# Queries, maxima and normalised rows issued from ScalarE's DMA queue in a decoder-layer kernel

## The chip, the cores and the metric

The kernel runs on one core of a Trainium2 chip. Its engines are TensorE (PE, with PEld for the loading of weights), VectorE (DVE), ScalarE (ACT), GpSimd (POOL) and SyncE (SP); SP does no arithmetic here and issues transfers. A transfer between DRAM and the on-chip memory (SBUF), or within SBUF, is issued by an instruction of SP, ACT or POOL, which stands in the order of that engine's other instructions. The metric is the device time of one execution in microseconds (us); less is better. Three runs of the kernel before took 1378.53, 1389.58 and 1391.62 us, a median of 1389.58 us.

## The reference

The input x has 16 batches of 128 positions and 1024 channels in float32, and a context of the same shape goes with it. Three residual blocks follow each other, each behind a layer normalisation:

```
x = x + attention(layernorm(x))        # 32 query heads of 32, 8 key heads, rope, causal softmax
x = x + autocorrelation(layernorm(x), ctx, ctx)
x = x + mixed_streams(layernorm(x))
```

The autocorrelation takes the correlation of each channel with the context's by Fourier transforms, keeps the nine largest delays, and adds the context shifted by them with softmax weights. The last block splits the channels into four streams of 256 and computes, per position, logits for a 4x4 matrix, which 50 Sinkhorn iterations make doubly stochastic; the matrix mixes the four streams, and a small matrix product of their weighted sum is added.

## The kernel before, in words

**First part.** Projections and rope are computed for four batches at a time. What the second part needs is written to DRAM: rotated queries (`qd`) and keys (`kd`), each as two float32 tensors whose sum is exact (a "high" and a "low" part), values (`vd`), and the spectra of the context (`sd`).

**Second part.** A Python generator `batch(b)` records the work of one batch in pieces, and each `yield` gives the time until the next piece. A heap merges the 16 generators (and `fill()`, which adds the last spectra) by these times, `PERIOD` = 33 apart; the merged order is the priority that a scheduler then works with when it writes each engine's instructions in one fixed list. On the chip every engine runs its own list in that order. Nothing overtakes on an engine, a transfer's issue included: an issue that waits for a semaphore holds up all that stands behind it on the same engine.

**Attention of a batch**, in two halves f of sixteen heads:

- `keys(b)` (L396 to L402) loads 96 rows of keys into one of two fixed buffers, the rows high, low, high, in three transfers from SP.
- `queries(b, f)` (L404 to L410) takes a buffer `qs` (two are in rotation) and loads the rows high, high, low, in three transfers of 256 KB from SP (L409). A product over the 96 rows is then the score to full precision.
- `maxima` multiplies queries by keys (L421), takes each row's maximum on DVE (L428), turns the 128x16 maxima into 16x128 by a TensorE transpose (L432), negates them into a rounded part `nh` on ACT (L434) and a rest `nl` on DVE (L436), writes both to DRAM from SP (L438), and reads them back from there into rows 96 and 97 of `qs` (L439). So the next product can subtract the maximum by itself.
- `attended` multiplies again in the other direction, now over all 98 rows (L447), takes the exponential on ACT (L451), masks on POOL (L452), and then sums the weights (L460) and the weighted values (L464) on TensorE. `batch(b)` loads the values (L786) behind the maxima.

**The rest of a batch.** `projected_out` (L507 to L509, 48 matmuls) adds to the rows of x in `xt` (three buffers, loaded at L793). `cross` multiplies the context's spectra with those of a sequence: a matmul (L516), a load `sv` of 512 KB (L518, two buffers in rotation), two ACT copies (L520, L521), a product on DVE (L523) and two on POOL (L524, L525). `delays` uses it once and `delayed` twice per half of the channels, six loads for a batch; between them stands the search for the nine largest (L541 to L562) on DVE. `logits` stores the row sums (L590), normalises into `z` on ACT (L162, L167), stores `z` to DRAM from SP (L593), and computes the logits (L603 to L615). `branch` adds the small product to the output by an accumulating transfer from POOL (L657). `sinkhorn` and `mixed` work on groups of 7, 6 and 3 batches; `mixed` reads the stored `z` back (L740), mixes on TensorE (L753) and adds to the output from POOL (L766).

**The order around the change.** All loads and stores of the second part but the accumulating ones stand on SP's list. With its waits, a batch has there: three issues of keys, six of queries, six of maxima, six of `sv`, and one each of values, x, row sums and `z`. ACT's list holds transfers only ahead of the second part (constants and weights).

Of the kernel before, what the change touches and what calls it, by code (L numbers as in the profile page):

```python
# [11 lines left out]
FP = mybir.dt.float32  # L12
FR = mybir.dt.float32r
# [7 lines left out]
B, L, D = 16, 128, 1024  # batches, positions, channels  # L21
NK = D // 128  # chunks of 128 channels
HD, NH, NKV = 32, 32, 8  # attention: head size, query heads, key heads
TG = 4  # batches that share one projection
# [3 lines left out]
TOPK = 9  # int(2 * ln(128))  # L28
ITERS = 50
REFRESH = 7  # L30
# [3 lines left out]
# The order of the program: us between batches, and between the parts of one.  # L34
PERIOD = 33
T_S, T_MX, T_M, T_ST, T_PT, T_SUM, T_DIV, T_OUT = 0, 3.29, 13.22, 1.0, 2.56, 54.8, 422239.83, 5.08
T_LN, T_X, T_DEL, T_TOP, T_WT, T_X2, T_DLD = 7.24, 5, 0, 9.35, 3.53, 2.3, 1.0
T_Z, T_ZT, T_LT, T_LOG, T_XP, T_XPT = 15, 2.82, 0.76, 8.03, 14.22, 1.18
SKS, MIXS = [45.0, 257.52, 400.81, 8, 8, 8], [11.22, 56.61, 24.78, 4, 4, 4]
# [8 lines left out]
T_FILL, T_SPEC = 39.7, 24.48  # L48
# [5 lines left out]
# The constant matrices, each [128, 128], in the order in which they lie in the input "mats".  # L54
# [4 lines left out]
def constant_matrices():  # L59
    """Rope tables, causal mask, and the real Fourier matrices of 128 positions.  # L60

    Rows 0..63 of a spectrum are real parts and rows 64..127 imaginary ones. At the even
    frequencies (k / 128) row 0 is frequency 0 and row 64 is frequency 64, both real; the odd ones
    are (k + 1/2) / 128. With a spectrum V of the context and one Q of the other sequence,
    V[re, re] * Q + V[im, im] * [Q im, -Q re] holds the real parts of a cross spectrum and, below
    them, its imaginary parts; at row 0 and 64 of the even frequencies V[im, im] is zero and
    V[re, re] has the real value.

    Frequency 0 adds the same to every correlation of a channel. Neither their order nor their
    softmax depends on it, so that "g" leaves it out, and "f_c" can add to frequency 0 the 128 of  # L70
    the last value by which the even half of the delayed sums lacks half the last value.
    """
# [18 lines left out]
    # Of the values less the last one.  # L91
# [9 lines left out]
    # Row 32 s + i to column i.  # L101
# [4 lines left out]
def constant_tokens():  # L106
    """Of row 4 t + j, one in column t."""
    return np.repeat(np.eye(32, dtype=np.float32), 4, 0)
# [3 lines left out]
def tile_decoder(ctx: ExitStack, tc, x, cx, wqkv, wo, wlog, base, gate, wb, mats, toks, zero, eye4, out):  # L112
# [11 lines left out]
    # What the first part leaves to the second: rotated queries and keys in two exact parts each,  # L124
    # values, and the context's spectra (even re, even im, odd re, odd im; each twice, below each other).
    qd = [dram.tile([TG, 2, 4, 2, 128, 128], FP, name=f"qd{g}") for g in range(B // TG)]
# [4 lines left out]
    def rsqrt(v, eps):  # L131
        """1 / sqrt(v + eps), with a Newton step behind the tables."""
# [13 lines left out]
    def layernorm(o, i):  # L146
        """Into o; the variance and the factor too."""
# [9 lines left out]
    def layernorm_act(o, i, sums, norm):  # L157
        """The same on ScalarE, of the sums of two halves."""
# [13 lines left out]
    def over(a, n):  # L172
        """[128, m] -> [128, m, n]"""
        return a.unsqueeze(2).to_broadcast([128, a.shape[1], n])

    def repeat(a, n):
        """[128, m] -> [128, n, m]"""
        return a.unsqueeze(1).to_broadcast([128, n, a.shape[1]])

# [1 line left out]
    # The last spectra fill the beginning of the second part: what they need lies to the right.  # L181
# [3 lines left out]
    with ExitStack() as att:  # L185
# [12 lines left out]
        def weights(j, n):  # L198
            """A block of 256 columns, half of its rows."""
# [39 lines left out]
        def rotated(xh, xl, col, d):  # L239
            """Two chunks of features, of the first and the second halves of eight heads."""  # L240
# [38 lines left out]
        def tokens(g):  # L279
            """Begun before the projections of the group before it are done."""  # L280
# [14 lines left out]
        # Keys, values, then queries.  # L295
# [11 lines left out]
        for g in range(B // TG):  # L307
# [6 lines left out]
            for p in range(4):  # L314
                more_weights(2)
                rotated(xh, xl, p * 256, qd[g][:, :, p])
                more_spectra(SPEC[g][p])
                ahead = next(coming, None)

# [7 lines left out]
    def q_late():  # L327
        """What the first batch needs behind the last spectra."""
# [36 lines left out]
    # The ninth largest, and no others.  # L365
# [15 lines left out]
    # sigmoid(gate), and (1 - sigmoid(gate)) on the diagonal.  # L381
# [12 lines left out]
    max_d = [[dram.tile([2, 16, 128], FP, name=f"mx{b}_{f}") for f in range(2)] for b in range(B)]  # L394

    def keys(b):  # L396
        g, t = divmod(b, TG)
        ks = KS[b % 2]
        rows = kd[g][t].rearrange("i u (d h) t -> i (u d) (h t)", h=8)
        for r, i in enumerate((0, 1, 0)):  # L400
            SP.dma_start(out=ks[32 * r : 32 * r + 32, :].bitcast(FP), in_=rows[i])
        return ks  # L402

    def queries(b, f):  # L404
        g, t = divmod(b, TG)
        qs = q2.tile([98, 2, 1024], FR, name="qs")
        rows = qd[g][t, :, 2 * f : 2 * f + 2].rearrange("i p u (d h) t -> i (u d) p (h t)", h=8)
        for r, i in enumerate((0, 0, 1)):
            SP.dma_start(out=qs[32 * r : 32 * r + 32].bitcast(FP), in_=rows[i])  # L409
        return qs.rearrange("r p c -> r (p c)")  # L410
# [470 lines left out]
```

## Time and profile before

| what | us |
|---|---|
| median of three runs | 1389.58 |
| span of the profiled execution, first to last instruction | 1391.9 |
| first part, to about | 390 |
| attention of batches 0 to 15, first to last maxima transpose | 414.3 to 1091.3 |
| logits of the last batch written (L615) | 1213.0 |
| last mixed stream added from POOL (L766) issued | 1383.9 |

| engine | busy us | share of the span |
|---|---|---|
| PE | 1134.1 | 81% |
| DVE | 874.0 | 63% |
| POOL | 673.0 | 48% |
| ACT | 580.5 | 42% |

The profile was taken in one execution; its span of 1391.9 us is 0.3 us above the longest of the three runs, so that nothing has to be added for what lies around it. A line of code is written L421, and an arrow `a<-b` reads "a is written from b". A busy PE is not PE at its limit, since the ends of pipelined matmuls are modelled: neighbouring matmuls of L507 to L509 are listed with 0.39 us each and start 0.23 us apart. DMA queue 1 carries what SP issues, 199.99 MB of 221.78 MB; ACT's queue 10 carries 3.90 MB.

### The profile page before, as it was taken

The page shows a single profiled execution, that of the slowest core. Times are in us where ns is not written, and L with a number is a line of the kernel's source. Part 1 is how long each engine was busy: PE and PEld are TensorE (multiplying, and loading weights), DVE is VectorE, ACT ScalarE, POOL GpSimd, SP SyncE. Part 2 cuts the span into 40 slices and gives each one's busy share as a digit, 9 for nine tenths or more (in the row PEclk, how much of TensorE's full clock was granted, in tenths as well). Part 3 has the DMA queues.
Part 4 walks back from the last instruction along what each step waited for, and adds up shares of the span by engine and source line. Part 5 has one row for each costly group of instructions (what it writes and reads, how often), then busy time and mean ns, then how long its engine had stood idle before and what let it go on. Part 6 is the DMA issues. An engine that isn't in the chain of part 4 may idle for free.

```text
span 1391.9 us, 17636 instructions
## 1 busy us (share of the span) xinstructions
PE 1134.1 (81%) x5024; PEld 725.9 (52%) x5024; DVE 874.0 (63%) x2910; ACT 580.5 (42%) x1281; POOL 673.0 (48%) x813
## 2 busy tenths in 40 slices
PE   5999969989847999999999998999998976452232
PEld 3888748758623555645565555645564553231121
DVE  5463332321123466977788778968897999986840
ACT  3331221221223355557565666556555755321010
POOL 0353313223413365565566656676766766643332
PEclk9999989989956999999999999999999987655555
DMA  6662864765898444576556664476455444365265
GB/s 227 213 215 84 229 204 123 229 196 137 245 271 250 123 129 140 156 200 166 152 161 170 194 180 135 131 183 156 145 158 153 123 119 115 87 121 106 49 121 76
DMA packets 141824, 221.78 MB, mean 159 GB/s; under 512 B 23264, under 2 KB 86112, under 8 KB 141664
## 3 DMA queue, kind: packets, MB, share of 16 engines
q1 hardware_dynamic: 127936, 199.99, 49.1%
q0 software_dynamic: 10752, 16.78, 8.4%
q10 hardware_dynamic: 3040, 3.90, 0.9%
q8 instruction: 39, 0.64, 0.2%
q14 instruction: 57, 0.47, 0.1%
HBM read 129.93 MB, written 90.83 MB: 159 GB/s over the span
## 4 chain that ended last, share of the span: by engine, by line
PE 40%; DVE 27%; DMA 16%; issue 6%; ACT 4%; SPq 4%; POOL 3%; POOLq 0%; DVEq 0%; ACTq 0%
PE mm L249 4%; PE mm L247 4%; PE mm L248 4%; PE sm L460 4%; PE av L464 3%; PE ps L516 3%; DMA sv<-sd 3%; DMA out<-mx 2%; DVE mx L428 2%; PE o L507 2%; DVE kept L542 2%; DMA sd<-F 2%; PE ps L227 2%; PE o L508 2%; DVE P L523 2%
## 5 line engine op out<-in xcount | busy, mean ns | idle before, releaser
L524 POOL TENSOR_TENSOR s<-s,sv 128x512 f32<-128x512 f32 x96 | 125.2, 1305 | 64.6 <-ACT s L521 47.3
L753 PE MATMUL ps<-mz,hm 128*128 128x256 f32 x128 | 59.4, 622 | 97.5 <-POOL hm L745 71.9
L525 POOL TENSOR_TENSOR P<-P,s 128x512 f32<-128x512 f32 x96 | 125.9, 1313 | 13.3 <-DVE P L523 11.6
L247 PE MATMUL mm<-xh,wh 128*128 128x512 f32 x320 | 131.2, 412 | 0.0
L248 PE MATMUL mm<-xl,wh 128*128 128x512 f32 x320 | 126.6, 396 | 0.2 <-DVE xl L216 0.2
L249 PE MATMUL mm<-xh,wl 128*128 128x512 f32 x320 | 125.5, 392 | 0.0
L257 POOL TENSOR_TENSOR ra<-ra,rb 128x512 f32<-128x512 f32 x40 | 50.4, 1279 | 155.3 <-DVE rb L256 155.2
L507 PE MATMUL o<-woh,ch 128*128 128x512 f32 x256 | 108.9, 425 | 8.3 <-DVE xt L500 6.1
L452 POOL TENSOR_SCALAR_AFFINE_SELECT pt<-pt 128x512 f32<-128x512 f32 x128 | 83.7, 668 | 64.7 <-ACT pt L451 63.0
L508 PE MATMUL o<-woh,cl 128*128 128x512 f32 x256 | 106.8, 417 | 4.7 <-POOL cl L494 4.7
L421 PE MATMUL sc<-ks,qs 96*128 96x128 f32 x512 | 98.2, 323 | 10.1 <-DMA qs<-qd 10.1
L228 ACT COPY F<-ps 128x512 f32<-128x512 f32 x64 | 36.5, 585 | 158.5 <-DMA sd<-F 85.5
L509 PE MATMUL o<-wol,ch 128*128 128x512 f32 x256 | 101.9, 398 | 0.0
L428 DVE TENSOR_REDUCE mx<-sc 128x4 f32<-128x512 f32 x128 | 86.4, 680 | 23.7 <-PE sc L421 23.7
L421 PEld LDWEIGHTS sc<-ks,qs 96*128 96x128 f32 x512 | 82.4, 204 | 33.0 <-issue 26.6
L753 PEld LDWEIGHTS ps<-mz,hm 128*128 128x128 f32 x128 | 36.0, 305 | 120.7 <-POOL hm L745 82.0
L523 DVE TENSOR_TENSOR P<-sv,ps 128x512 f32<-128x512 f32 x96 | 64.8, 675 | 52.6 <-ACT s L521 38.1
L227 PE MATMUL ps<-raw,am 128*128 128x512 f32 x128 | 71.1, 681 | 30.6 <-ACT F L228 25.7
L451 ACT ACTIVATE pt<-sc 128x512 f32<-128x512 f32 x128 | 73.7, 598 | 31.5 <-PE sc L447 30.5
L460 PE MATMUL sm<-pt,ones 128*32 128x512 f32 x256 | 79.7, 617 | 1.9 <-POOL pt L452 1.9
L520 ACT COPY s<-ps 64x512 f32<-64x512 f32 x96 | 56.0, 583 | 55.9 <-PE ps L516 40.2
L516 PE MATMUL ps<-wT,bm 128*128 128x512 f32 x128 | 70.8, 638 | 9.3 <-ACT wT L571 8.9
(171 smaller groups left out, 2852.3 us busy)
## 6 DMA issues: line engine op xcount, KB each, us to landing
sv<-sd SPq DMA_DIRECT2D x96, 512.0 KB
qs<-qd SPq DMA_DIRECT2D x96, 256.0 KB
sd<-F SPq DMA_DIRECT2D x80, 256.0 KB
xt<-in_x SPq DMA_DIRECT2D x32, 512.0 KB
out<-mx POOLq DMA_DIRECT2D x32, 512.0 KB, 5.9
sd<-F SPq DMA_DIRECT2D x48, 252.0 KB
raw<-in_cx SPq DMA_DIRECT2D x16, 512.0 KB
qd<-hi SPq DMA_DIRECT2D x32, 256.0 KB
```

What stands on the lines that cost most here:

```text
L247: PE.matmul(ps, lhsT=wh[:, k, c], rhs=h, start=k == 0, stop=False)
L248: PE.matmul(ps, lhsT=wh[:, k, c], rhs=r, start=False, stop=False)
L249: PE.matmul(ps, lhsT=wl[:, k, c], rhs=h, start=False, stop=k == NK - 1)
L421: PE.matmul(sc[:, j, :], lhsT=qs[0:96, h * 128 : (h + 1) * 128], rhs=ks[0:96, g * 128 : (g + 1) * 128], start=False, stop=j == 3,)
L428: DVE.tensor_reduce(mx[:, 4 * s : 4 * s + 4], sc, AX.X, ALU.max)
L460: PE.matmul(sm[32 * s : 32 * s + 32, :], lhsT=ones, rhs=pt, start=True, stop=True)
L507: PE.matmul(ps, lhsT=h, rhs=woh[:, k, cols], start=k == 0, stop=False)
L508: PE.matmul(ps, lhsT=r, rhs=woh[:, k, cols], start=False, stop=False)
L509: PE.matmul(ps, lhsT=h, rhs=wol[:, k, cols], start=False, stop=k == NK - 1)
L516: PE.matmul(ps, lhsT=M[m], rhs=of, start=True, stop=True)
L524: POOL.tensor_mul(s, s, v[:, 1, :])
L525: POOL.tensor_add(P, P, s)
```

## The change

Comments and docstrings go, and four things change in the second part:

1. The queries of batch b + 1 are loaded inside `attended` of batch b, from ACT, behind the last exponential of the half that read the buffer's old content; only those of batch 0 are loaded by SP. They come in two transfers, 32 and 64 rows, which the layout of `qd` now allows. Keys stay on SP, in two transfers of 64 and 32 rows.
2. Both parts of the negated maxima lie in one tile `nm`, and each goes straight from there into its row of `qs` by one transfer from ACT. The DRAM tensors `max_d` are gone.
3. The store of `z` is issued by ACT.
4. Some of the times between pieces are others.

```diff
-T_S, T_MX, T_M, T_ST, T_PT, T_SUM, T_DIV, T_OUT = 0, 3.29, 13.22, 1.0, 2.56, 54.8, 422239.83, 5.08
-T_LN, T_X, T_DEL, T_TOP, T_WT, T_X2, T_DLD = 7.24, 5, 0, 9.35, 3.53, 2.3, 1.0
+T_S, T_MX, T_M, T_ST, T_PT, T_SUM, T_DIV, T_OUT = 0, 4.95, 13.22, 1.0, 2.56, 13.96, 422239.83, 5.08
+T_LN, T_X, T_DEL, T_TOP, T_WT, T_X2, T_DLD = 8.24, 5, 0, 9.35, 3.53, 2.82, 1.0
-SKS, MIXS = [45.0, 257.52, 400.81, 8, 8, 8], [11.22, 56.61, 24.78, 4, 4, 4]
+SKS, MIXS = [45.0, 257.52, 400.81, 8, 8, 8], [11.22, 56.61, 25.82, 4, 4, 4]
-T_FILL, T_SPEC = 39.7, 24.48
+T_FILL, T_SPEC = 39.7, 32.17
...
-    qd = [dram.tile([TG, 2, 4, 2, 128, 128], FP, name=f"qd{g}") for g in range(B // TG)]
+    qd = [dram.tile([TG, 4, 2, 2, 128, 128], FP, name=f"qd{g}") for g in range(B // TG)]
...
-                rotated(xh, xl, p * 256, qd[g][:, :, p])
+                rotated(xh, xl, p * 256, qd[g][:, p])
...
-        rows = kd[g][t].rearrange("i u (d h) t -> i (u d) (h t)", h=8)
-        for r, i in enumerate((0, 1, 0)):
-            SP.dma_start(out=ks[32 * r : 32 * r + 32, :].bitcast(FP), in_=rows[i])
+        rows = kd[g][t].rearrange("i u (d h) t -> (i u d) (h t)", h=8)
+        SP.dma_start(out=ks[0:64, :].bitcast(FP), in_=rows)
+        SP.dma_start(out=ks[64:96, :].bitcast(FP), in_=rows[0:32])
...
-    def queries(b, f):
+    def queries(b, f, eng):
         g, t = divmod(b, TG)
         qs = q2.tile([98, 2, 1024], FR, name="qs")
-        rows = qd[g][t, :, 2 * f : 2 * f + 2].rearrange("i p u (d h) t -> i (u d) p (h t)", h=8)
-        for r, i in enumerate((0, 0, 1)):
-            SP.dma_start(out=qs[32 * r : 32 * r + 32].bitcast(FP), in_=rows[i])
-        return qs.rearrange("r p c -> r (p c)")
+        rows = qd[g][t, 2 * f : 2 * f + 2].rearrange("p i u (d h) t -> (i u d) p (h t)", h=8)
+        eng.dma_start(out=qs[0:32].bitcast(FP), in_=rows[0:32])
+        eng.dma_start(out=qs[32:96].bitcast(FP), in_=rows)
+        coming[b, f] = qs.rearrange("r p c -> r (p c)")
...
-        nh = q2.tile([16, 128], FR, name="nh")
-        ACT.activation(nh, tp, AF.Copy, scale=-1.0)
-        nl = q2.tile([16, 128], FR, name="nl")
-        DVE.scalar_tensor_tensor(nl, tp, -1.0, nh.bitcast(FP), ALU.mult, ALU.subtract)
-        for i, o in enumerate((nh, nl)):
-            SP.dma_start(out=max_d[b][f][i], in_=o.bitcast(FP))
-        SP.dma_start(out=qs[96:98, :].bitcast(FP), in_=max_d[b][f].rearrange("i h t -> i (h t)"))
+        nm = q2.tile([16, 2, 128], FR, name="nm")
+        ACT.activation(nm[:, 0], tp, AF.Copy, scale=-1.0)
+        DVE.scalar_tensor_tensor(nm[:, 1], tp, -1.0, nm[:, 0].bitcast(FP), ALU.mult, ALU.subtract)
+        for i in range(2):
+            ACT.dma_start(
+                out=qs[96 + i : 97 + i, :].bitcast(FP).rearrange("i (h t) -> i h t", h=16), in_=nm[:, i].bitcast(FP)
+            )
...
             pts.append(pt)
+            if s == 3 and b + 1 < BATCHES:
+                queries(b + 1, f, ACT)
             yield T_ST
...
-        SP.dma_start(out=zd[b], in_=z)
+        ACT.dma_start(out=zd[b], in_=z)
...
-            QS.append(queries(b, f))
+            if b == 0:
+                queries(b, f, SP)
+            QS.append(coming.pop((b, f)))
```

More of the change, by code (lines that the diff above doesn't have):

```diff
@@ L393, in tile_decoder @@
     scale = 1.0 / math.sqrt(HD)
-    max_d = [[dram.tile([2, 16, 128], FP, name=f"mx{b}_{f}") for f in range(2)] for b in range(B)]
     def keys(b):
@@ L398, in keys @@
         ks = KS[b % 2]
-        rows = kd[g][t].rearrange("i u (d h) t -> i (u d) (h t)", h=8)
-        for r, i in enumerate((0, 1, 0)):
-            SP.dma_start(out=ks[32 * r : 32 * r + 32, :].bitcast(FP), in_=rows[i])
+        rows = kd[g][t].rearrange("i u (d h) t -> (i u d) (h t)", h=8)
+        SP.dma_start(out=ks[0:64, :].bitcast(FP), in_=rows)
+        SP.dma_start(out=ks[64:96, :].bitcast(FP), in_=rows[0:32])
         return ks
-    def queries(b, f):
+    def queries(b, f, eng):
         g, t = divmod(b, TG)
         qs = q2.tile([98, 2, 1024], FR, name="qs")
-        rows = qd[g][t, :, 2 * f : 2 * f + 2].rearrange("i p u (d h) t -> i (u d) p (h t)", h=8)
-        for r, i in enumerate((0, 0, 1)):
-            SP.dma_start(out=qs[32 * r : 32 * r + 32].bitcast(FP), in_=rows[i])
-        return qs.rearrange("r p c -> r (p c)")
+        rows = qd[g][t, 2 * f : 2 * f + 2].rearrange("p i u (d h) t -> (i u d) p (h t)", h=8)
+        eng.dma_start(out=qs[0:32].bitcast(FP), in_=rows[0:32])
+        eng.dma_start(out=qs[32:96].bitcast(FP), in_=rows)
+        coming[b, f] = qs.rearrange("r p c -> r (p c)")
+    coming = {}
     def maxima(b, ks, qs, f):
```

## The prediction

> **What bounds the kernel now.** I read the busy time by stretches first, to find the stage that the change touches; then the chain that ended last inside one batch's period; then who waits for the links of that chain. Columns: length, busy time and instruction count of PE, PEld, DVE, ACT, POOL, granted clock, DMA share, GB/s.
>
> ```profile
> 500.00:680.00 180.00, 170.39 (x793) 99.52 (x792) 136.03 (x434) 107.73 (x240) 106.99 (x108) 0.99 0.59 163
> 680.00:900.00 220.00, 209.43 (x1018) 122.80 (x1016) 178.69 (x573) 135.53 (x303) 140.46 (x154) 1.00 0.60 167
> ...
> 1115.00:1230.00 115.00, 70.81 (x251) 40.75 (x250) 111.81 (x487) 52.01 (x130) 71.21 (x115) 0.74 0.39 103
> 1230.00:1392.00 162.00, 54.06 (x116) 32.05 (x114) 85.80 (x437) 20.24 (x48) 52.76 (x103) 0.53 0.54 95
> ```
>
> From 500 to 1115 us no engine is full: DVE 81% of 680 to 900, ACT 62%, and PE's 95% is partly modelled ends. It is a net of in-order lists that wait for each other. From 1115 on DVE is 97% busy, then Sinkhorn's serial steps and the mixing follow; they hang on the last batch's logits at 1213.0 and take 178.9 us to the end, and the change leaves them as they are. So the gain or loss is made before 1115 and passes through to the end.
>
> The chain inside one period (start, length, what):
>
> ```profile
> 738.42 0.02 issue
> 738.44 0.30 SPq L409
> ...
> 741.67 5.97 DMA sv<-sd
> ...
> 747.77 0.69 DVE P L523
> ...
> 768.69 4.05 DMA mx<-nl
> ...
> 772.80 2.00 DMA qs<-mx
> 774.80 0.14 issue
> 774.93 0.47 PE sc L447
> ```
>
> The next period's `sv` stands at 785.34, so a batch takes 43.7 us. Two links are of the kind that the change cuts: 3.25 us in which SP issues three queries and three keys ahead of `sv` (738.42 to 741.67), and 6.1 us of maxima through DRAM (768.69 to 774.80). But a chain names one link at a time and not how close the next is. That is told by the idle time just before the waiting instructions:
>
> ```profile
> 747.77 0.69 DVE L523 TENSOR_TENSOR P<-sv,ps 128x512 f32<-128x512 f32 x1 [1.02 <-DMA sv<-sd]
> 774.93 0.47 PE L447 MATMUL sc<-qs,ks 98*128 98x512 f32 x1 [0.40 <-DMA qs<-mx]
> ```
>
> and by the waits summed over 500 to 1115 (total, times, longest):
>
> ```profile
> PE sc L447 <- DMA qs<-mx: 7.4, 6, 3.3
> DVE P L523 <- ACT s L521: 38.1, 25, 2.9
> DVE lg L615 <- PE ps L614: 16.6, 11, 4.5
> DVE P L523 <- DMA sv<-sd: 4.9, 6, 1.9
> POOL s L524 <- DMA sv<-sd: 14.9, 8, 4.3
> ```
>
> **The change, part by part.**
>
> *Maxima.* Gone per part: two SP issues, 4.05 us of writing, one issue, 2.00 us of reading. Added: two ACT issues and a transfer within SBUF. No row shows such a one. It goes into the same rows as qs<-mx (1.86 to 4.57 us in the chain) from the same sixteen as mx<-nl (2.98 to 4.79); by the typical rows it lies between 2.0 and 4.1, and I take 2.0, as nothing is written to DRAM. The link falls from 6.1 to 2.0. Of these 4.1 us the trace pays out little: behind the wait of 0.40 us stands PE's own list, whose previous product (L447) began at 774.04. All 32 parts together made PE wait 7.4 us directly. **−7**; nothing, if ACT issues late; −4.1 x 15 periods = −62 at the very most.
>
> *SP's list.* Per batch 12 issues go to ACT or vanish (six queries, six maxima) besides one of the keys and z's. Ahead of `sv` two keys remain, 2 x 0.46 = 0.9 us, so it is issued 2.35 us earlier. The hold-up itself stays: the keys still wait for the last L447 of the half, as the queries did (SP spent 82.7 us at L409 on it), and `sv` still stands behind them; x's load, which now waits for z by itself because z's reader frees its buffer, holds SP as z's store did. And in the period at 785.34 it was POOL, freeing the buffer, that released `sv`. So I count the waits for `sv`, 4.9 on DVE and 14.9 on POOL, and take half, **−10**; bounds 0 and −20.
>
> Does a second queue let `sv` overtake the queries? In the packets of the trace the 4 KB ones of queries and keys run to 744.8, and then come the 2 KB ones of `sv`, to 748. The Trainium skill ("DMA: Bandwidth & Descriptors", "Issuing engines are not separate DMA queues") says no: all queues end on the same 16 DMA engines and interleave, and a further issuing engine saves its issue time alone. By the rule this part is worth at most the 2.35 us of issue per batch; if `sv` overtook, 5 us. Either is more than the 1.02 us for which DVE waited, so the sum is the same.
>
> *ACT's list.* It gets 4 x 15 queries, 4 x 16 maxima and 16 stores, 140 issues, at 0.33 to 0.39 us (its own constants) or 0.42 (SP's queries). An issue runs beside the copy ahead of it:
>
> ```profile
> 380.25 0.59 ACT L228 COPY F<-ps 128x512 f32<-128x512 f32 x1 [1.87 <-DMA sd<-F]
> 380.27 0.37 ACTq L359 DMA_DIRECT2D eye_sb<-in_eye  x1
> 380.73 0.62 ACT L259 CAST hi<-ra 128x512 fp32r<-128x512 f32 x1
> ```
>
> so a single one costs little and the second of a pair shows. Behind what do they stand, in the new list? The first half's maxima come before the four L557, for which ACT waited 5.12 us anyway; the second half's before the first exponential, 0.7 us, and ACT idled 0.96 us right after that one (before 769.35). `nl` ends at 768.13, about when the first issue is through, so the added wait is small. The queries have no cover: the first pair falls into 7 us in which ACT works without a break (769.35 to 776.42), behind it the next half's exponentials and then PE's L460; the second pair stands before an exponential too. Per batch 2 x 0.42 + 0.35 = 1.2 us on the path, x 16 = **+19**; bounds 0 and all issues, (4 x 0.35 + 4 x 0.42 + 0.34) x 16 = +55.
>
> *Order.* PE's list in a period is nearly the old one. ACT's and DVE's are not: the squares of z's normalisation and its 1/sqrt now stand before the second half's search instead of behind it, so z is ready sooner. ACT waited 11.6 us (L167) and 16.6 us (L162) for DVE's means, DVE 16.6 us for the logits that follow z; and DVE's 38.1 us for the copies `s` shrink when the products ahead of them are not held up. Of 16.6 + 38.1 I take 40%, **−22**; the same sort of reshuffle can lose as much, so bounds −40 and +20.
>
> *Beginning.* At 437.32 three issues (3.07 us in all) and a 5.76 us load of batch 1's queries are on the chain, behind SP's stores of spectra. From ACT, behind the exponential, it is one issue less and no store before it: **−4**, bounds 0 and −8.
>
> Sum: −7 − 10 + 19 − 22 − 4 = −24 on 1391.9 = 1368. The median of the runs is 2.3 us under that span: **1366**.
>
> **Rivals.**
>
> *It is hidden anyway* (25%). For it: 0.40 and 1.02 us of real waiting against links of 6.1 and 3.25; against it, the summed waits. The queries may also leave no sooner than before, as they now stand behind exponentials in ACT's list. Then −7 − 10 − 4 + 19 and nothing from the order: −2, 1388 on the median.
>
> *The whole links count* (10%): near-critical neighbours shrink too, as they wait for the same products. 4.1 + 2.35 − 1.2 = 5.2 us x 15 = −78, 1312. DVE's idle 8 us of a period would allow it; the 0.40 speaks against.
>
> *ACT becomes the gate* (20%, slower). Its copies and exponentials sit between PE and everything, and POOL (45.2 us) and DVE (38.1) wait for `s` already. Place: the stretch 767 to 785. If every issue lands on the path (3.4 us a batch, 55) and the order gives nothing, 55 − 21 = +34: 1423. It decides once more than 1.3 us a batch (21 / 16) of ACT's issues are uncovered. The eight transfer semaphores in rotation are now shared by both queues, so an ACT issue can also wait for an SP transfer; in the steady period those were issued some 18 us before (values at 749.53 for the maxima at 767), which covers it.
>
> **How the numbers follow.** Forecast case 45%, 1350 to 1380. About 1% (14 us) is what a measurement of this kernel can tell from no change. Faster by over that: 0.40 of the forecast and the 0.10 of the whole links, 0.50. Slower: the 0.20, and 0.02 of the hidden case. Same: 0.28. The range 1325 to 1415 takes in hidden and forecast cases and leaves out about 0.06 below and 0.12 above.
>
> **What would show it.** Right: no wait of L447 for maxima that last over 3 us, a transfer into `qs` rows of about 2 us; SP's waits at maxima gone; a period of about 42.3 us between the `sv` links; DVE's wait for `s` under 30. Wrong: a period over 43.7, ACT rows behind the issues as new releasers of PE, POOL waits for `s` over 45, or an end more than 179 us behind the last logits.

## The result, and the profile after

The changed kernel took a median of 1398.7 us beside 1392.8 us of the kernel before, twenty runs of each: a ratio of 1.0058, with a 95% interval of 1.0042 to 1.0075. So it is not 1.7% faster, as forecast, but some 0.6% slower. Its profiled execution has a span of 1396.7 us. One of the nine executions of mix_qz, a kernel of the experiments below, was slow (3782.1 us), and its ratio there leaves this one out.

The busy time by stretches, in the columns of the prediction (length; busy time and count of PE, PEld, DVE, ACT, POOL; granted clock, DMA share, GB/s), of the kernel after:

```profile
500.00:680.00 180.00, 176.09 (x832) 101.91 (x830) 135.26 (x443) 116.06 (x254) 110.65 (x112) 1.00 0.58 171
680.00:900.00 220.00, 211.56 (x1000) 124.16 (x1001) 173.86 (x599) 134.29 (x300) 138.41 (x161) 1.00 0.56 161
1115.00:1230.00 115.00, 72.94 (x261) 40.55 (x260) 107.47 (x429) 52.65 (x128) 63.26 (x92) 0.78 0.36 97
1230.00:1392.00 162.00, 53.23 (x120) 31.74 (x120) 92.59 (x461) 21.48 (x50) 54.21 (x106) 0.56 0.56 99
```

From 500 to 680 us the kernel after is ahead (832 matmuls of PE against 793, 443 instructions of DVE against 434). From 680 to 900 it has done 18 matmuls fewer, but 26 instructions of DVE more, and its clock is as full. So DVE gets small instructions here that stood elsewhere before, at a full clock; its busy time is not longer (173.86 us against 178.69).

The waits from 500 to 1115 us (total, times, longest) of the kernel after. Those for `s`, `sv`, `lg` and `qs` answer to the lines of the prediction; the others grew:

```profile
POOL s L528 <- ACT s L525: 34.5, 27, 3.7
ACT pt L452 <- PE sc L448: 33.3, 21, 3.6
...
DVE P L527 <- ACT s L525: 31.2, 18, 2.7
ACT ch L496 <- DVE c L480: 26.1, 16, 3.9
...
ACT z L162 <- DVE mean L160: 22.8, 12, 4.1
...
POOL s L528 <- DMA sv<-sd: 12.9, 6, 2.8
...
DVE kept L566 <- POOL corr L565: 9.9, 12, 1.2
...
DVE s L711 <- POOL P L716: 7.0, 12, 1.6
...
DVE s L714 <- POOL P L713: 6.4, 11, 1.0
...
DVE lg L619 <- PE ps L618: 3.2, 3, 1.7
...
PEld sc L448 <- DMA qs<-nm: 0.7, 1, 0.7
```

Almost every wait that the prediction named is shorter: for the maxima 0.7 us instead of 7.4, DVE for `s` 31.2 instead of 38.1, DVE for the logits 3.2 instead of 16.6, POOL for `sv` 12.9 instead of 14.9. These four alone are 29 us less, and the time has not fallen. About the same time now stands at other waits: exponentials behind their product 33.3 (21.8 before), `ch` 26.1 (18.9), z 22.8 (16.6). And two lines are of a kind that the prediction did not look for: steps of the Sinkhorn iterations on DVE (L711, L714) that wait for POOL, 13.4 us together where it was 5.3. The lines of the kernel before are:

```profile
ACT pt L451 <- PE sc L447: 21.8, 16, 3.6
...
ACT ch L492 <- DVE c L476: 18.9, 16, 4.1
...
ACT z L162 <- DVE mean L160: 16.6, 12, 3.3
...
DVE s L710 <- POOL P L709: 3.9, 7, 1.0
...
DVE s L707 <- POOL P L712: 1.4, 3, 0.5
```

Where the time goes is seen best batch by batch, by the start of each batch's logits on DVE (L615, in the kernel after L619). All times in us, from the profiled executions. "Batch 0" runs from the first transposed maxima to the first logits, the tail from the last logits to the end:

| kernel | batch 0 | 0 to 7 | 7 to 13 | 13 to 15 | tail |
|---|---|---|---|---|---|
| before | 143 | 314.4 | 278.6 | 63.2 | 178.9 |
| after | 134 | 313.8 | 292.5 | 63.5 | 177.9 |

So in these two executions the change gains 9 us in batch 0, nothing in the seven periods that follow, and loses 14 us from batch 7 to 13. The tail is what the prediction said (178.9 against 177.9).

### The profile page after: what moved, and what is told of

Same layout as the page of the kernel before. It is cut to its first block, busy times and chain, and to the rows that moved or that the text cites. A ratio compares the mean times of both kernels' runs of the same rounds, so it can differ in the third digit from the quotient of the medians.

```text
span 1396.7 us, 17570 instructions
## 1 busy us (share of the span) xinstructions
PE 1135.5 (81%) x5024; PEld 725.7 (52%) x5024; DVE 880.1 (63%) x2910; ACT 583.7 (42%) x1281; POOL 670.7 (48%) x813
## 5 line engine op out<-in xcount | busy, mean ns | idle before, releaser
L528 POOL TENSOR_TENSOR s<-s,sv 128x512 f32<-128x512 f32 x96 | 128.1, 1335 | 56.1 <-ACT s L525 40.0
L757 PE MATMUL ps<-mz,hm 128*128 128x256 f32 x128 | 56.2, 592 | 99.9 <-POOL hm L749 69.7
L529 POOL TENSOR_TENSOR P<-P,s 128x512 f32<-128x512 f32 x96 | 126.1, 1317 | 15.5 <-DVE P L527 9.7
L453 POOL TENSOR_SCALAR_AFFINE_SELECT pt<-pt 128x512 f32<-128x512 f32 x128 | 82.9, 669 | 63.5 <-ACT pt L452 63.3
L227 PE MATMUL ps<-raw,am 128*128 128x512 f32 x128 | 69.6, 668 | 28.1 <-ACT F L228 26.1
L527 DVE TENSOR_TENSOR P<-sv,ps 128x512 f32<-128x512 f32 x96 | 64.8, 675 | 42.4 <-ACT s L525 32.3
L464 PE MATMUL sm<-pt,ones 128*32 128x512 f32 x256 | 84.5, 646 | 4.2 <-DVE mx L627 2.2
L261 POOL TENSOR_TENSOR lo<-ra,hi 128x512 fp32r<-128x512 f32 x40 | 52.1, 1310 | 57.8 <-ACT hi L259 57.7
```

What stands on the lines that cost most here:

```text
L464: PE.matmul(sm[32 * s : 32 * s + 32, :], lhsT=ones, rhs=pt, start=True, stop=True)
L528: POOL.tensor_mul(s, s, v[:, 1, :])
L529: POOL.tensor_add(P, P, s)
L757: PE.matmul(ps[:, k, :], lhsT=hm[:, 2 * h + k].rearrange("p t i -> p (t i)"), rhs=z[:, 2 * h + k, :], start=True, stop=True,)
```

## The experiments

Each ratio is to executions of the kernel before that were taken together with it; their median was 1393 to 1397 us. The stretches are those of the table above.

| kernel | ratio (95% interval) | batch 0 | 0 to 7 | 7 to 13 | 13 to 15 | tail |
|---|---|---|---|---|---|---|
| after | 1.0058 (1.0042–1.0075) | 134 | 313.8 | 292.5 | 63.5 | 177.9 |
| after_oldtimes | 1.0311 (1.0263–1.0359) | 134 | 345.9 | 298.2 | 64.8 | 178.0 |
| before_newtimes | 1.0098 (1.0062–1.0133) | 133 | 329.3 | 283.2 | 64.2 | 178.8 |
| after_allSP | 0.9999 (0.9977–1.0022) | 136 | 315.3 | 281.8 | 61.7 | 180.5 |
| before_qACT | 1.0101 (1.0064–1.0137) | 135 | 321.3 | 280.4 | 68.2 | 180.6 |
| before_g0short | 1.0009 (0.9989–1.0029) | 140 | 314.6 | 304.0 | 60.7 | 155.7 |
| after_g0short | 0.9978 (0.9955–1.0000) | 133 | 313.4 | 304.4 | 62.5 | 156.6 |
| after_qSP | 1.0047 (1.0028–1.0067) | 136 | 318.2 | 281.1 | 62.1 | 184.0 |
| after_mSP | 1.0106 (1.0083–1.0130) | 144 | 312.5 | 286.3 | 66.5 | 180.0 |
| before_g0empty | 0.9911 (0.9881–0.9940) | 139 | 314.5 | 269.9 | 64.2 | 176.6 |
| after_g0empty | 0.9936 (0.9915–0.9957) | 137 | 315.3 | 276.7 | 64.0 | 177.9 |
| after_x2 | 1.0048 (1.0028–1.0068) | 132 | 327.8 | 278.6 | 63.9 | 181.5 |
| before_mSP | 0.9981 (0.9959–1.0003) | 140 | 309.7 | 275.1 | 67.1 | 183.5 |
| fix_allSP | 1.0076 (1.0049–1.0103) | 133 | 318.2 | 294.2 | 63.6 | 182.4 |
| fix_qSP | 1.0087 (1.0054–1.0119) | 133 | 319.9 | 290.9 | 62.5 | 182.4 |
| fix_mSP | 1.0012 (0.9993–1.0030) | 134 | 311.6 | 290.1 | 63.6 | 181.2 |
| dbl_all | 1.0074 (1.0046–1.0101) | 135 | 314.1 | 297.9 | 62.4 | 179.9 |
| mix_qz | 1.0038 (1.0007–1.0068) | 136 | 314.9 | 281.5 | 62.0 | 184.1 |
| mix_q | 1.0025 (1.0005–1.0046) | 138 | 313.7 | 282.6 | 61.8 | 181.6 |

How far such a number is to be trusted is seen where lists are the same. Up to batch 7 before_g0short and before_g0empty have the list of the kernel before: 314.6, 314.5 and 314.4 us. For the kernel after it is 313.4, 315.3 and 313.8. So a difference of under 2 us in a stretch means nothing. Batch 0 scatters more (139 to 143 us with the list of the kernel before, 133 to 137 with that of the kernel after), and so does the tail. A row's stretches come from one execution, its ratio from six or more: that of before_qACT was its fastest (1401.5 us, where the median was 1408.8).

### Transfers and times apart

```diff
 after_oldtimes: the kernel after with the times of before
-T_S, T_MX, ... T_SUM = 0, 4.95, ... 13.96    (and the other changed times)
+T_S, T_MX, ... T_SUM = 0, 3.29, ... 54.8
 before_newtimes: the kernel before with those of after
```

> The changed kernel with the times between pieces of the kernel before, so the transfers alone. Its DVE list has 34, 32, 36, 36 Sinkhorn steps of the first group between the logits of batches 7 to 11 (before: 26, 23, 25, 27; changed: 28, 37, 35, 36). Crowding theory (the loss of 8 to 10 us around batches 8 to 10 comes from these steps standing denser): slower than before by 5 to 15 us, loss in the same place. Theory of the times (the new times made the loss): equal to before or up to 10 us faster. ACT theory (issues on ACT's list lengthen every period): slower by 5 to 15 us, but spread over batches 3 to 12 at about 1 us each.

> The kernel before with the new times alone; transfers are the old ones, Sinkhorn steps 26, 23, 25, 24. Theory of the times: slower by 5 to 10 us. Crowding and ACT theories: within 4 us of the kernel before.

Measured: 3.1% slower and 1.0% slower, both outside what was expected: the first lost 42 us where no theory had more than 15, and most of it before batch 7. Each half of the change by itself is worse than both together. The stretch from batch 0 to 7 takes 345.9 us with the one and 329.3 with the other, against 314: the same work on the same engines, put into other lists. The kernel after has the transfers of after_oldtimes and takes 313.8: with the same transfers from the same engines, the times alone make 32 us in seven periods. All that they do is set the order, and the order is a term as large as anything that the transfers can bring.

### Who issues, in the scheduler's own order

```diff
 after_allSP
-                queries(b + 1, f, ACT)
+                queries(b + 1, f, SP)
-            ACT.dma_start(                       # maxima
+            SP.dma_start(
-        ACT.dma_start(out=zd[b], in_=z)
+        SP.dma_start(out=zd[b], in_=z)
 after_qSP: the first of these alone; after_mSP: the second alone
 before_qACT: before, with the queries' and keys' part of the change alone
 before_mSP: before, with the maxima's direct transfers alone, from SP
```

> The changed kernel with queries, maxima and z issued by SP at the same places: the new shapes of the transfers and no round trip through DRAM, but nothing on ACT. Sinkhorn steps 26, 27, 32, 26. ACT theory: faster than before by 5 to 15 us, since the round trip is gone and no issue stands on ACT's list, with a period of 43 us or less. Crowding theory: within 5 us of before, with the middle batches (8 to 10) near 47 us each. Rival to both: SP's hold-ups come back (queries wait for products ahead of the maxima), slower by 5 or more.

> Queries from ACT and keys and queries in two transfers alone, on the kernel before with its times; maxima through DRAM and z from SP. Sinkhorn steps 26, 26, 26, 28. ACT theory: the queries' issues, 0.32 and 0.63 us in the profile of the changed kernel, cost about 1 us a batch: 5 to 15 us slower than before minus about 8 us of gain at the beginning, so -5 to +7. Crowding theory: the gain at the beginning (8 to 10 us) stays, 5 to 10 us faster than before.

> The kernel after with the next batch's queries issued by SP instead of ACT, at the same place of the program; maxima and z stay on ACT. 60 issues of 0.32 and 0.63 us (28 us) leave ACT's list. Theory of ACT's issues: the queries are the uncovered ones, about half of that comes back, 1385. Crowding theory: its list has 30 25 27 23 Sinkhorn steps in batches 8 to 11 instead of 37 35 36 26, so 8 to 11 us come back as well, 1388. If only the maxima's issues (32 pairs of 1.58 us, the first exponential behind them) cost, the time stays at 1398.

> The kernel after with the maxima's two transfers issued by SP; queries and z stay on ACT. 64 issues of 0.54 us leave ACT's list. If the pair ahead of the first exponential is what costs (1.58 us against 0.24, of that some 0.2 to 0.4 us on the path, 32 times): 1387 to 1393. Against it, SP's issue stands behind its waits (sv, keys, x), and the maxima come late: then PE's wait for them comes back with 7 us or more, 1400 to 1410. Crowding theory: 28 35 26 26 steps, about half of the 11 us, 1393.

> The kernel before with the maxima alone sent straight from the tile to their rows of the queries' buffer, by two transfers that SP issues; queries, keys, z and all times as in the kernel before. The forecast gave this part 7 us (PE's summed waits for the maxima): 1387. If the link is hidden, 1393 to 1396. Its list has 27 22 26 26 Sinkhorn steps in batches 9 to 12, near those of the kernel before, so crowding plays no part.

Measured: with everything on SP the kernel is as fast as before (0.9999), and with everything on ACT it is at 1.0058; but with the maxima alone on SP it is at 1.0106. Read as costs of issues this makes no sense: the maxima would be better on ACT by 0.5%, and all three together better on SP by 0.6%. Each of these kernels has lists of its own. before_qACT fell where neither theory had it, at 1.0101. after_qSP takes 281.1 us from batch 7 to 13, as the crowding theory wants, but 318.2 before that, and its time is that of the third case, where nothing comes back. And after_mSP is 7.4 us ahead of the kernel after from batch 0 to 13, but 10 us behind in batch 0 (144 against 134); the runs do not show why.

before_mSP is the cleanest, since its lists are near those of the kernel before, though not the same. It saves 4.7 us from batch 0 to 7 and 3.5 to batch 13, gives back 3.9 in the two last periods and 4.6 in the tail, and its time is 0.19% less with an interval that just takes in no change. In this one execution the maxima's link is thus worth 0.5 to 0.7 us a batch while the pipeline runs. PE's list shows a reason for so little. From the end of the transpose of a half's maxima (L432) to the start of its own first product over 98 rows (L447) pass, in the second half of batches 5 to 9, 7.1 to 7.6 us in the kernel before, 6.9 in before_mSP and 7.1 to 7.5 in the kernel after; in the first half it is 16.0 to 19.7 us in the three. Other matmuls stand between, and most of the transfer lies beside them, direct or through DRAM. The waits for `sv` in before_mSP, of the view of the waits from 500 to 1115 us, did not shrink either:

```profile
POOL s L524 <- DMA sv<-sd: 17.6, 9, 4.4
DVE P L523 <- DMA sv<-sd: 5.4, 7, 1.7
```

Though six issues of maxima on SP became four, the load `sv` that stands behind them is waited for as long as before (14.9 and 4.9).

### Crowded Sinkhorn steps

The first group's Sinkhorn iterations (batches 0 to 6) begin once batch 6's logits are there, and are small steps on DVE and POOL between the instructions of the next batches. In DVE's list, the periods that end with the logits of batches 8, 9 and 10 hold 23, 25 and 27 of them in the kernel before, but 37, 35 and 36 in the kernel after. The groups of instructions of DVE from the logits of batch 7 to those of batch 10 (busy, mean ns of one | idle time before them, what ended it), first of the kernel before in 871 to 1012 us:

```profile
L710 DVE TENSOR_REDUCE s<-P 128x28 f32<-128x112 f32 x17 | 5.9, 344 | 1.3 <-POOL P L709 1.1
L708 DVE RECIPROCAL r<-s 128x28 f32<-128x28 f32 x17 | 5.4, 317 | 0.1
L711 DVE RECIPROCAL r<-s 128x28 f32<-128x28 f32 x17 | 5.4, 315 | 0.1
...
L707 DVE TENSOR_REDUCE s<-P 128x28 f32<-128x112 f32 x17 | 4.4, 256 | 1.4 <-ACT P L702 1.0 <-POOL P L712 0.4
```

and of the kernel after in 863 to 1015 us:

```profile
L714 DVE TENSOR_REDUCE s<-P 128x28 f32<-128x112 f32 x24 | 8.2, 343 | 4.2 <-POOL P L713 4.1
L715 DVE RECIPROCAL r<-s 128x28 f32<-128x28 f32 x24 | 7.7, 322 | 0.3
L712 DVE RECIPROCAL r<-s 128x28 f32<-128x28 f32 x24 | 7.7, 319 | 0.2
...
L711 DVE TENSOR_REDUCE s<-P 128x28 f32<-128x112 f32 x24 | 6.2, 260 | 4.8 <-POOL P L716 4.0 <-ACT P L706 0.8
```

24 iterations instead of 17, and DVE waits 9.0 us in front of their sums (L711, L714) instead of 2.7, nearly all of it for POOL's products. The busy time of those three periods, kernel before, then after:

```profile
871.00:1012.00 141.00, 133.56 (x619) 76.14 (x619) 118.22 (x405) 84.38 (x191) 98.83 (x133) 0.99 0.57 155
```

```profile
863.00:1015.00 152.00, 135.97 (x618) 78.55 (x616) 133.70 (x445) 84.40 (x196) 103.42 (x151) 0.96 0.51 146
```

PE and ACT do the same work in 152 us as in 141, DVE 15.5 us more; PE's clock is a little lower (0.96 against 0.99). DVE is not full even so: its 133.7 us of work and 9.0 us of these waits leave 9 of 152. To test it, the steps were taken away, once with the mixing of the group moving forward (short), once with the times between the pieces kept (empty), so that the mixing stays at the end:

```diff
 before_g0short, after_g0short
-        for block in range((ITERS - 1) // REFRESH):
+        for block in range(1 if gi == 0 else (ITERS - 1) // REFRESH):
 before_g0empty, after_g0empty
         for block in range((ITERS - 1) // REFRESH):
+            if gi == 0 and block:
+                yield SKS[gi]
+                continue
```

> The kernel before with the Sinkhorn iterations of the first group cut to the first of seven blocks: 36 blocks' worth of small steps of DVE, POOL and ACT between batches 8 and 15 is left out, so part of the computation is missing and only the difference to the same cut in the kernel after counts. Crowding theory (the order packs these steps into batches 8 to 11 of the kernel after): this kernel gains 10 to 25 us on the kernel before, spread over batches 8 to 15. Theory of ACT's issues: the same here.

> The kernel after with the same cut. Crowding theory: the beginning's 8 us stay and the losses of 11 us at batches 8 to 10 and of 5 at 12 go, so it is 6 to 10 us faster than the other cut kernel. Theory of ACT's issues: those are all still there, so it remains 3 to 6 us slower than the other, or the loss moves to other batches.

The short pair misled in its detail. The first kernel gained nothing on the kernel before (1.0009), where 10 to 25 us were expected: the group's 56 mixing matmuls then stand between the logits of batches 8 and 11, and both kernels take 304 us from batch 7 to 13. Still the kernel with the change is now the faster of the two, by 0.31% or 4 us, where 6 to 10 were expected.

> The kernel before with six of the seven blocks of the first group's Sinkhorn iterations left out (part of the computation is missing), but with their times between pieces kept, so that the mixing of that group stays behind the last logits, as in both full kernels. Crowding theory: the stretch from the logits of batch 7 to those of batch 13 (278.6 us in the kernel before) falls by 0 to 10 us.

> The kernel after with the same cut. Crowding theory: the stretch from batch 7 to 13 (292.5 us in the kernel after, 14 more than before) falls to within 3 us of the other cut kernel's, and as batch 0 ends some 7 us earlier, the time is 5 to 9 us below the other's. Theory of ACT's issues: they are all still there, the difference of 10 us or more in this stretch stays.

The empty pair, same three periods, before_g0empty and then after_g0empty:

```profile
870.00:1011.00 141.00, 130.77 (x613) 75.60 (x612) 108.00 (x344) 81.62 (x184) 84.06 (x91) 0.96 0.58 154
```

```profile
870.00:1012.00 142.00, 130.68 (x613) 76.85 (x612) 107.21 (x348) 82.55 (x186) 83.35 (x90) 0.96 0.57 157
```

Without the steps both take 141 to 142 us, at the lower clock too. The kernel before doesn't gain a microsecond there by leaving out 10 us of DVE's work. The kernel after gains 10 of its 11 us. That is what crowding forecasts, and the lower clock alone does not make the loss. But it is not proof: the scheduler wrote new lists for both, and from batch 7 to 10 the traces show the other instructions of DVE, ACT, POOL and PE in another order than in the full kernels. So the steps were not taken away alone.

The orders of all the kernels say the same, with the same weakness. Counted like the 75 steps of the kernel before from batch 7 to 10, eight orders have 72 to 87 (before, before_newtimes, before_mSP, before_qACT, after_allSP, after_qSP, after_mSP, after_x2) and take 134.4 to 143.5 us there; the two with over 100 (after with 108, after_oldtimes with 104) take 152.2 and 154.2. Whether the steps' time on DVE, POOL's products or the waits between them make it was not told apart.

From batch 10 to 13 the empty pair keeps a difference (128.7 and 134.5 us) that crowding by the first group can't be. The whole stretch from 7 to 13 differs by 6.8 us, between the two expectations, and the time of after_g0empty is 0.25% above the other's, where 5 to 9 us below were expected. What makes that rest stays open.

```diff
 after_x2
-T_LN, T_X, T_DEL, T_TOP, T_WT, T_X2, T_DLD = 8.24, 5, 0, 9.35, 3.53, 2.82, 1.0
+T_LN, T_X, T_DEL, T_TOP, T_WT, T_X2, T_DLD = 8.24, 5, 0, 9.35, 3.53, 2.3, 1.0
```

> The kernel after with one time between pieces set back (T_X2 2.82 to 2.3). All transfers and issues are those of the kernel after; the list of DVE then holds 27 25 25 28 Sinkhorn steps in batches 9 to 12 instead of 37 35 36 26. Crowding theory: the stretch from batch 7 to 13 falls from 292.5 to 278 to 285 us, and the time to some 1388. Theory of ACT's issues: the stretch stays at 290 or more, the time at 1396 to 1400. If another order by itself costs, batches 0 to 7 (313.8) get longer too.

One time, set back by 0.52 us, spreads the steps, and the stretch from 7 to 13 falls to 278.6 us, exactly that of the kernel before, with all 140 issues still on ACT. But batches 0 to 7 grow by 14.0 us: the new list takes with one hand what it gives with the other.

### The issues alone, with every list held

The next four kernels are edited behind the scheduler. PE, DVE and POOL run the lists of the kernel after instruction for instruction, and so does ACT but for what is moved or added; in the traces they stand in the same order from batch 0 to 13. The edits are given in short form.

```diff
 fix_allSP, fix_qSP (queries only), fix_mSP (maxima only), run on the finished lists
+if i.engine == eng.Activation and type(i).__name__ == "InstDMACopy" and name in MOVED:
+    kept += i.sync_info.on_wait                     # these waits stay on ACT's next instruction
+    waits = [*i.sync_info.on_wait, reached(ACT, n)]  # and SP waits for ACT to be there
+    i = copy.replace(i, engine=eng.SP, queue="qSPDynamicHW", sync_info=...)
 dbl_all
+for _ in range(2):                                   # behind each of ACT's 140 transfers
+    todo.append(a copy of one column on ACT, without a wait or a signal)
```

> The kernel after with the lists of PE, DVE, POOL and ACT left instruction for instruction as they are (the edit is made behind the scheduler): only the 140 issues of queries, maxima and z are taken out of ACT's list and put at the same places into SP's, where each waits for ACT to have reached that place; the waits themselves stay on ACT too. Some 69 us of issues leave ACT. The forecast's term for ACT (1.2 us of a batch on the path, 19 in all): 1380. If ACT's issues are covered and the order alone makes the time: 1396 to 1401. If what they hold up in SP's list (sv, keys, x stand behind them there) costs more than ACT's time: 1403 to 1415.

> The same with the 60 issues of queries alone moved to SP, all lists otherwise those of the kernel after. The forecast held these for the uncovered ones (0.84 us of a batch): 1386. Covered: 1396 to 1401.

> The same with the 64 issues of maxima alone moved to SP. The forecast's term was 0.35 us of a batch: 1393. With the measured 0.5 us for each, and the pair ahead of an exponential: 1385. Covered: 1396 to 1401. If they come late from SP, PE waits for the maxima: over 1403.

> The kernel after, all lists as they are, with two copies of one column (some 0.2 us each) put into ACT's list behind each of the 140 transfers that it issues in the second part, about as much as the issues themselves take: 57 us more work on ACT, 3.6 us a batch. The forecast's term for ACT: 16 to 19 us more, 1416. The rival that makes ACT the gate: up to 55 more, 1450. If ACT has room for it: no more than 5, 1398 to 1404.

Measured, beside the 1.0058 of the kernel after: 1.0076, 1.0087, 1.0012, 1.0074. To take all issues from ACT does not help; if anything it costs. The first three forecasts of a covered issue had 1396 to 1401 us; reckoned from the ratios on the 1392.8 us of the first comparison they are 1403, 1405 and 1394, so only the last came in. From batch 0 to 13 the kernel after takes 606.3 us, fix_allSP 612.4, fix_qSP 610.8 and fix_mSP 601.7. So in this list the queries are better on ACT by 4.5 us, and the maxima worse by 4.6. The parts do not add up, since all together are better on ACT by 6.1 us; z, or what the parts do to each other, was not told apart. That of the maxima is shown by the times too (the intervals 0.9993 to 1.0030 and 1.0042 to 1.0075 are apart, 6 us); that of the queries only by the stretches of one execution. Here the Trainium skill bears on the case ("DMA: Bandwidth & Descriptors", "Issuing engines are not separate DMA queues"): a second issuing engine saves the issue time alone, which it calls usually small beside the transfer itself. The runs agree that the whole move is small (fix_allSP to the kernel after 2.5 us). Of its parts, that of the maxima has the other sign.

Doubling ACT's issues with copies of 0.19 us changed nothing from batch 0 to 7 (314.1 against 313.8) and cost 5.4 us from 7 to 13, all of it from batch 7 to 10 (157.7 us against 152.2; then 140.2 in both). The busy time of the whole stretch, kernel after and then dbl_all:

```profile
500.00:1115.00 615.00, 583.95 (x2717) 334.93 (x2715) 497.60 (x1657) 377.12 (x841) 401.81 (x488) 0.99 0.54 159
```

```profile
498.00:1113.00 615.00, 581.69 (x2698) 336.73 (x2697) 494.48 (x1644) 394.07 (x1063) 395.82 (x482) 0.98 0.55 158
```

222 more instructions on ACT, some 42 us by their mean, of which the busy time shows 17 (the rest lay inside what was busy), and 19 matmuls fewer of PE. So ACT has room for this but in the three crowded periods.

These kernels make a row of steps: from the kernel before to after_allSP nothing (ratio 0.9999); from after_allSP to fix_allSP, which have the same transfers from the same engine and differ in the order (and in the waits that fix_allSP keeps), +0.77% or 10.7 us, with 15.3 us from batch 0 to 13; from fix_allSP to the kernel after, which have the same order, −0.18% or 2.5 us, within the uncertainty. By this row the loss is the order's. By another it is not: fix_mSP has the order of the kernel after too, and with the maxima alone on SP its time is that of the kernel before (1.0012). The next kernels give a second pair to judge the order by.

### The two halves put together

If the queries and z are better on ACT and the maxima on SP, the order of after_allSP, which has no crowding, should gain by them.

```diff
 mix_qz: the lists of after_allSP, with queries and z moved behind the scheduler from SP's list to ACT's (short form)
 mix_q: with the queries alone
+if i.engine == eng.SP and type(i).__name__ == "InstDMACopy" and name in MOVED:
+    i = copy.replace(i, engine=eng.Activation, queue="qActDynamicHW")
```

> The order that the scheduler gives when SP issues everything (after_allSP: 1394.7, no crowding of Sinkhorn steps), all its lists kept, and behind the scheduler the queries and z moved from SP's list to the same places of ACT's; the maxima stay on SP. In the order of the kernel after, the same difference (fix_mSP against fix_allSP) was 0.64%, 9 us. If that holds in this order too: 1385 to 1389 beside a kernel before of 1394, faster than both kernels. If the gain belongs to the other order alone: 1393 to 1397.

> The same with the queries alone moved to ACT and z left on SP. In the order of the kernel after the queries' part was 4 us (after against fix_qSP): 1390. If z is what holds SP's list, this one stays at 1394 and the other kernel has the gain.

Measured: 1.0038 and 1.0025, no gain; both are a little above even the cases without one (up to 1397 us and 1394 us; by the ratios they are at 1400 and 1398). From batch 0 to 13 the three take 597.1, 596.4 and 596.3 us. In this order it does not matter who issues the queries. The 4.5 us of fix_qSP belong to the other list; why there, no run shows.

mix_qz and fix_mSP have the same issuers (queries and z on ACT, maxima on SP) and differ in the order and in the waits that the moves keep. From batch 7 to 13 they take 281.5 and 290.1 us; with all on SP it was 281.8 and 294.2 (after_allSP, fix_allSP). So the longer stretch goes with the order, by 8.6 and 12.4 us, whoever issues. In the whole time only the pair with all on SP shows it: mix_qz is at 1.0038 and fix_mSP at 1.0012, with intervals that overlap. So the order alone is not shown to make the kernel slower, nor is the maxima's issue alone, since no run has the order of after_allSP with the maxima on ACT. Shown is that no loss of the whole time can be told in fix_mSP, which has that order without the maxima on ACT (its stretch from 7 to 13 stays 11.5 us longer than in the kernel before), nor in after_allSP, which has neither.

No complete kernel here beats the one before beyond doubt.

## Why the prediction was wrong

**The failing step is the order.** It took 40% of the waits for logits and for `s` as time, −22 us, with bounds of −40 and +20. These waits did shrink, by 20.3 us, and no time came of it: with the same issuers the new order takes 8.6 to 12.4 us more from batch 7 to 13 than that of after_allSP, and with all issues on SP 10.7 us more in the whole time. So the sign was wrong. A wait that goes is not time saved here; ACT waited 24.9 us longer instead, for products, `c` and the means of L162. The bound of +20 held it, the value taken did not. The measured 1398.7 us lie in the stated range because the range is wide enough for a loss; the direction was not foreseen.

**What was overlooked is where the loss is.** The prediction looked at Sinkhorn's steps only behind the last logits, and read the stretch of 680 to 900 us as typical of the rest. DVE's idle 8 us of a period were counted as room for the whole-links rival. The first group's steps use that room from batch 7 on, and where the order puts 36 of them into a batch instead of 25 the periods are 11 us longer in three. That the steps themselves make it is likely, and not shown by an edit that changes nothing else.

**Maxima, −7.** The waits fell by 6.7 us. What the direct transfer itself takes, 2.0 us by the prediction, stands in no view of the kernel after. Alone the part gave some 2.6 us of time (an interval from a loss of 0.4 to a gain of 5.7), and in the kernel after the issuing from ACT took 6 us. The step had the reason that halves it in its own text: PE's list stands ahead of the product.

**SP's list, −10, and ACT's list, +19.** Together +9; held at the same order, the move from SP to ACT measured −2.5 us. Of ACT's 19 us, 13.4 were the queries', which at the same order are not better on SP (fix_qSP), and 5.6 the maxima's, which is about what fix_mSP gives back; that is partly luck, as an issue was taken for 0.35 us and is 0.54. Work on ACT by itself is cheap: as many copies again cost nothing in seven periods. The second transfer of queries was longer than assumed too (0.63 us instead of 0.42). The gain on SP's side is real in one order (4.5 us for the queries, in one execution) and absent in another. The wait for `sv` on POOL fell by 2.0 us only; on DVE the 4.9 us are gone from the list, but 4.3 us of the same instruction's waits are put down to the maxima there, which it does not read.

**Beginning, −4.** Batch 0 is 9 us shorter in the two profiles, and some 6 by all that share their lists. Whether for the reason given is open: with the times of before, the queries' part alone gives 135 us, but before_newtimes, which leaves the queries on SP, gains the same (133 us), and so does after_allSP (136).

**Rivals.** The nearest is that it is hidden anyway: from batch 0 to 7 it is right to the microsecond (314.4 and 313.8 us), though with terms (−10, +19) that were not measured so. It forecast 1388 for the whole, since it gave the order nothing. ACT as the gate is refuted by dbl_all (up to 6 us from batch 0 to 13, not 55) and by POOL's wait for `s`, which fell to 34.5 us instead of rising over 45. (Its sum, 1389.6 + 34, is 1424 and not 1423.)

**The signs.** The waits of PE for the maxima (0.7 us left) and of SP at them are gone, and DVE's wait for `s` came near its mark (31.2 us, where under 30 was asked). The period did not follow: 44.4 to 44.6 us from batch 1 to 6, where 42.3 was forecast and over 43.7 was to tell the forecast wrong. The first signs showed that the waits at the links were cut, not that they were on the path.

## What to carry to other kernels

Where a scheduler writes the lists, each edit is two edits: the one meant, and a new order. Judge the first with the lists held (move or double the instructions behind the scheduler), and compare periods beside whole times, since with the same list those between the logits of batches 0 and 6 repeat to 0.6 us or better here. A whole time can still say otherwise, as mix_qz and fix_mSP do. Count background work per period against the idle time of its engine before the change and after it: here three periods took 134 to 144 us in the orders with 24 to 29 small steps in each on the mean, and 152 to 154 us in those with 35 or 36. And price an edit by what stands ahead of the waiting instruction in its own engine's list, not by the waits that it removes.

## What the runs showed of the hardware

The time of an issue depends on the transfer's form more than on the engine. By the lines of the code, in the kernel after (min, median and max in ns):

```profile
L438 ACTq DMA_DIRECT2D qs<-nm x64: 510/540/957, 419.1 to 1094.1; - x64
L407 ACTq DMA_DIRECT2D qs<-qd x30: 309/319/388, 436.4 to 1064.2; - x30
L408 ACTq DMA_DIRECT2D qs<-qd x30: 602/632/1792, 436.8 to 1064.6; - x30
```

and in fix_mSP, where SP issues the maxima:

```profile
L439 SPq DMA_DIRECT2D qs<-nm x64: 503/517/1347, 419.1 to 1089.4; - x64
```

A transfer of 8 KB from sixteen rows into one row takes longer to issue (0.54 us) than a load of 256 KB to 32 rows (0.32), and 512 KB to 64 rows take twice as long as that. SP needs about the same as ACT for the same transfer. To make two transfers of three therefore saved little: 0.32 + 0.63 us instead of three of 0.42.
